# LayerNorm chains of a deformable-convolution block kept with pixels on partitions

## The chip, the cores and the metric

The kernel runs on one core of one Trainium2 chip. Its time is the device time of one execution in microseconds (us), lower is better. A time is given as the median of several runs, and one further execution was recorded by the hardware profiler.

The engines are named as in the profile: PE (TensorE matmul), PEld (its weight loads), DVE (VectorE), ACT (ScalarE), POOL (GpSimd) and SP (SyncE, which issues DMAs). PE, DVE and ACT each run their own list of instructions in order.

## What is computed

The input x is float32 of shape (2, 256, 128, 128): two images, 256 channels. Two residual layers follow each other; `_gn` is a group norm with 32 groups and no weights.

```python
def _ln2d(x, w, b):                      # over channels, at each pixel
    u = x.mean(1, keepdims=True)
    s = ((x - u) ** 2).mean(1, keepdims=True)
    return w[None, :, None, None] * (x - u) / jnp.sqrt(s + EPS) + b[None, :, None, None]

def _branch(x, w_off, w_def, lw, lb, pad, dil):
    off = _conv(x, w_off, pad, dil)              # 18 offsets at each pixel
    y = _deform_dw(x, off, w_def, pad, dil)      # 9 bilinear samples, depthwise weights
    return gelu(_ln2d(y, lw, lb))

# layer 0, on x = _gn(x)
x1, x2, x3 = (_branch(x, ..., dil) for dil in (1, 9, 12))
c = einsum('bchw,oc->bohw', x, conv_w) + conv_b
out = _ln2d(x1 + x2 + x3 + c, n1_w, n1_b)
h = gelu(out^T @ mlp_w1.T + mlp_b1) @ mlp_w2.T + mlp_b2      # 256 -> 512 -> 256
x = x_in + _ln2d(h^T + out, n2_w, n2_b)
# layer 1: x = x + 3x3 convolution of _gn(x) with ternary weights, + bias
```

In the inputs all norm weights (bw, n1_w, n2_w) are ones and all norm biases (bb, n1_b, n2_b) are zeros; conv_b, mlp_b1 and mlp_b2 are random.

## The kernel before

It has three stages. Phase A reads x, takes the first group norm's statistics, writes a padded table of pixels to DRAM, computes the offsets, and stores "hats" (the interpolation weights along y and x) in DRAM. The largest offset decides between two paths (`far`, `flag`, `beyond`): the near path `sample_near`, which these inputs take, and a general path `sample_any`, which gathers pixel by pixel with indirect DMAs. Phase C is layer 1's convolution, and neither its code nor its inputs' shapes are touched.

**Sampling.** `sample_near` walks 270 units: 2 images, 45 rows of tiles (`Rt`), 3 branches. A unit has two samples, one for each half of the 256 channels (`c`), so a row of tiles has six samples. A sample is up to 17 products of a pixel tile `xs` (126 pixels x 128 channels, the stationary operand) with a sampling matrix `A` of 216 columns or fewer (L933). Their results land in four PSUM banks `pm` (two tiles to a bank), ACT copies them to `ev` (L953, two buffers), and DVE adds them with the depthwise weights into a ring of image rows, one ring for each branch (L903). The matrix `A` of a unit is built by DVE in three steps, each a product of two hats `h` (L847); `HBUFS` hat buffers are loaded ahead on SP's queue, 567 KB each. The 17 `xs` tiles of a row of tiles are loaded on POOL's queue (L783) into `XBUFS` = NT + 6 = 23 buffers, so 6 loads of the next row can go at once, and the others wait until the current row's last sample has released its tiles.

**The tail.** When four image rows of a branch are complete in its ring, a chain begins for this group `g` of 512 pixels (`Tail.branch`). There are 64 groups, each with a chain for every branch. A chain is a Python generator: `yield n` means "go on n ticks later", and `yield n, k` also names how many of `VBUFS` tiles the chain holds then. `Tail.advance` is one tick; each sample has three, before its first product and at the tiles of `TICKS` = (5, 11). So the tail's instructions are laid between the sampling products of PE, and between ACT's copies and DVE's sums, in the order that the ticks give; `pin` keeps it.

Each chain normalises over channels in `Tail.normalised`. The data lie with channels on partitions, so it transposes eight 128x128 blocks on PE into two PSUM banks (L603, tile `tp`), lets ACT copy them to SBUF (L608, tile `T`), takes mean and variance with DVE (L616, L618), computes scale and shift with four small POOL operations (L620 to L623, tile `rs`), scales on ACT (L627, four instructions of 256 columns), and transposes the eight blocks back on PE (L639, tile `zc`). The branch then applies GELU with the norm's weights from `zc` on ACT (L655, two instructions of 512 columns). Branch 0 stores its result in DRAM (`g12d`), branch 1 adds its own (L669), and branch 2 loads the sum (`other`), loads the group's x again (`xn`), subtracts the mean on ACT (L678) and goes on in `Tail.finish`: 1x1 convolution (L583, `pc1`, products of 512 columns), sums on DVE (L695, L699), the norm with n1 (L705), the MLP's two products (L583, `hp` and `h2`) with GELU between them on ACT (L718) and the sum on DVE (L733), the norm with n2, and the residual sum (L754) with statistics for the second group norm (L758). A group so has five norms: three in the branches, two in `finish`.

All PSUM tiles of the tail (`tp`, `zc`, `pc1`, `hp`, `h2`) share one tag of four banks; with the four `pm` banks, PSUM's eight are in use. Up to `NORMS` = 3 chains may be within a norm at once.

Of the kernel before, what the change touches and what calls it, by code (L numbers as in the profile page):

```python
# [9 lines left out]
F32 = mybir.dt.float32  # L10
I32 = mybir.dt.int32
U32 = mybir.dt.uint32
BF16 = mybir.dt.bfloat16
AF = mybir.ActivationFunctionType
ALU = mybir.AluOpType
AX = mybir.AxisListType
# [3 lines left out]
P = 128  # L20
W = 128
C = 256
KC = C // P
HID = 512
MC = HID // P
R = 4
NG = R * W
# [7 lines left out]
LN_EPS = 1e-6  # L35
# [5 lines left out]
LIMIT = float(REACH)  # L41
RI, CI = 3, 8
TR, TC = RI + 2 * REACH, CI + 2 * REACH
NT = -(-(W + 2 * REACH) // CI)
# [8 lines left out]
RINGS = (9, 25, 31)  # L53
BRS = (0, 1, 2)
NORMS = 3
VBUFS = 9
PEAK = 3
GAP = 2
LAG = 5
XBUFS = NT + 6  # L60
HBUFS = 4
EBUFS = 2
TICKS = (5, 11)
XCLS = (0, 1, 4, 7)
# [10 lines left out]
def conv_preact_kernel(ctx: ExitStack, tc: tile.TileContext, t: dict, out: bass.AP):  # L75
    nc = tc.nc
    x = t["x"]
    NB, _, H, _ = x.shape
# [5 lines left out]
    const = ctx.enter_context(tc.tile_pool(name="const", bufs=1))  # L84
    scratch = ctx.enter_context(tc.tile_pool(name="scratch", bufs=1, space=DRAM))
    small = ctx.enter_context(tc.tile_pool(name="small", bufs=2))


    ident = const.tile([P, P], F32, name="ident")
# [3 lines left out]
    mhalf = const.tile([P, NG // P], F32, name="mhalf")  # L93
# [9 lines left out]
    def load_now():  # L103
        for tl, src in later:
            nc.sync.dma_start(tl, src)
        later.clear()
# [3 lines left out]
    convs = [  # L110
        load(f"convw{b}", [P, KC, C], t["convw"].rearrange("(k p) o -> p k o", p=P))
        for b in range(NB)
    ]
    negmean = [const.tile([P, KC], F32, name=f"negmean{b}") for b in range(NB)]
    w1 = load("w1", [P, KC, HID], t["w1"].rearrange("(k p) o -> p k o", p=P))
    w2 = load("w2", [P, MC, C], t["w2"].rearrange("(k p) o -> p k o", p=P))
    defw = load("defw", [P, KC, NTAP], t["defw"].rearrange("(k p) t -> p k t", p=P))
    bw = load("bw", [P, 3, KC], t["bw"])
    bb = load("bb", [P, 3, KC], t["bb"])
    b1 = load("b1", [P, MC], t["b1"])  # L120
    b2 = load("b2", [P, KC], t["b2"])
    convb = load("convb", [P, KC], t["convb"])
    n1w = load("n1w", [P, KC], t["n1w"])
    n1b = load("n1b", [P, KC], t["n1b"])
    n2w = load("n2w", [P, KC], t["n2w"])
    n2b = load("n2b", [P, KC], t["n2b"])
    l1b = load("l1b", [P, KC], t["l1b"])


    wpn = const.tile([P, 2], F32, name="wpn")  # L130
    for i, name in enumerate(("wp", "wn")):
# [8 lines left out]
    def dram(name, shape):  # L140
# [7 lines left out]
    g12d = dram("g12d", [C, HW])  # L148
    x1d = dram("x1d", [C, HW])
# [3 lines left out]
    stats2 = [  # L153
        const.tile([P, KC, NGRP, 6], F32, name=f"stats2_{b}", tag=f"stats2_{b}") for b in range(NB)
    ]
# [301 lines left out]
    with ExitStack() as actx:  # L457
        psum = actx.enter_context(tc.tile_pool(name="ps_a", bufs=1, space=PSUM))

        def gps():  # L460
            return psum.tile([P, 512], F32, name="gnps", tag="tp", bufs=2)

        ap = actx.enter_context(tc.tile_pool(name="apool", bufs=1))
        dxs = sorted({d * s for d in DILS for s in (-1, 0, 1)})
        k = {
            "dxs": dxs,
            "zero": ap.tile([P, C], F32, name="zero"),
            "wz": ap.tile([P, KC, NZ], F32, name="wz"),
            "shift": ap.tile([P, len(dxs), P], F32, name="shift"),
            "hatw": ap.tile([P, 2, NTAP * NH], BF16, name="hatw"),  # L470
            "parts": [ap.tile([P, 2, ZG, P], BF16, name=f"parts{i}") for i in range(2)],
            "zr": ap.tile([P, ZRING, NZ], F32, name="zr"),
            "planes": [ap.tile([P, 2, NG], BF16, name=f"planes{i}") for i in range(RI)],
        }
        nc.vector.memset(k["zero"], 0.0)
        for parts in k["parts"]:
            nc.vector.memset(parts, 0.0)
        XT = min(4, NGRP)
        beside = store_signs(ap)
        for b in range(NB):  # L480
            stats = ap.tile([P, KC, NGRP, 6], F32, name=f"stats1_{b}", tag=f"stats1_{b}")
            for c in range(KC):
                for g0 in range(0, NGRP, XT):
                    xt = ap.tile([P, XT * NG], F32, name="xt", tag="xt", bufs=3)
                    nc.sync.dma_start(
                        xt,
                        x[b, c * P : (c + 1) * P].rearrange("p h w -> p (h w)")[
                            :, g0 * NG : (g0 + XT) * NG
                        ],
                    )  # L490
                    for j in range(XT):
                        nc.vector.bn_stats(stats[:, c, g0 + j, :], xt[:, j * NG : (j + 1) * NG])
            if b == 0:
                load_now()
                nc.sync.dma_start(k["wz"], t["wz"].rearrange("(k p) n -> p k n", p=P))
                nc.sync.dma_start(k["shift"], t["shift"])
                hatw = ap.tile([P, 2, NTAP * NH], F32, name="hatw32", tag="xt", bufs=3)
                nc.sync.dma_start(hatw, t["hatw"])
                nc.vector.tensor_copy(k["hatw"], hatw)
                pattern = ap.tile([P, RI, NG], F32, name="pattern", tag="xt", bufs=3)  # L500
                nc.sync.dma_start(pattern[HALF : HALF + NPAT], t["pattern"])
                for i, pl in enumerate(k["planes"]):
                    nc.vector.tensor_copy(
                        pl[HALF : HALF + NPAT, 1, :], pattern[HALF : HALF + NPAT, i]
                    )
            mean, rstd = group_norm(stats, f"gn1_{b}", gps)
            gn1.append((mean, rstd))

            nc.vector.tensor_scalar(negmean[b], mean, -1.0, None, ALU.mult)
            for c in range(KC):  # L510
                nc.vector.tensor_scalar(
                    convs[b][:, c, :], convs[b][:, c, :], rstd[:, c : c + 1], None, ALU.mult
                )
            phase_a(b, ap, psum, k, beside)
        for _ in beside:
            pass


    far = small.tile([P, 1], F32, name="far", tag="far")
    nc.vector.tensor_reduce(far, amax, AX.X, ALU.max)  # L520
    farall = small.tile([P, 1], F32, name="farall", tag="farall")
    nc.gpsimd.partition_all_reduce(farall, far, P, bass.bass_isa.ReduceOp.max)
    flag = const.tile([P, 1], I32, name="flag")
# [11 lines left out]
    class Tail:  # L535
# [10 lines left out]
        def begin(self, chain, wait):  # L546
            self.waiting.append([self.now + wait, chain, 0, 1])
# [28 lines left out]
        def bank(self, name):  # L576
            return self.psum.tile([P, 512], F32, name=name, tag="tl", bufs=4)
# [67 lines left out]
        def branch(self, b, br, g, y):  # L645

            pin = self.pin
            cols = slice(g * NG, (g + 1) * NG)
            gv = g12d[b].rearrange("(k p) f -> p k f", p=P)[:, :, cols]
            z = []  # L650
            yield from self.normalised(z, y, (b, br, g))
            v = z[0]
            for c in range(KC):
                pin(
                    nc.scalar.activation(  # L655
                        v[:, c, :], z[1 + c], AF.Gelu,
                        scale=bw[:, br, c : c + 1], bias=bb[:, br, c : c + 1],
                    )
                )
            if br == 0:  # L660
                yield 2
                nc.sync.dma_start(gv, v)
                return
            yield 1, 1 + br
            other = self.tile("other")
            nc.sync.dma_start(other, gv)
            if br == 1:
                yield 2
                pin(nc.vector.tensor_tensor(v, v, other, ALU.add))  # L669
                yield 2  # L670
                nc.sync.dma_start(gv, v)
                return
            xn = self.tile("xn")
            nc.sync.dma_start(xn, x[b].rearrange("(k p) h w -> p k (h w)", p=P)[:, :, cols])
            yield 2
            for c in range(KC):
                pin(
                    nc.scalar.activation(  # L678
                        xn[:, c, :], xn[:, c, :], AF.Identity, bias=negmean[b][:, c : c + 1]
                    )  # L680
                )
            yield 1
            yield from self.finish(b, g, v, other, xn)
# [78 lines left out]
            )  # L762


    def sample_near(pool, psum, k):

        pin = tc.keep_in_program_order
        tail = Tail(pool, psum, pin)
        units = [(b, Rt, br) for b in range(NB) for Rt in range(NR) for br in BRS]
        xts, hbs, owners, begun = {}, {}, {}, set()  # L770
        done = {(b, br): 0 for b in range(NB) for br in BRS}
# [191 lines left out]
        for u, (b, Rt, br) in enumerate(units):  # L963
# [5 lines left out]
            while done[b, br] < NGRP and (  # L969
# [3 lines left out]
                g = done[b, br]  # L973
# [99 lines left out]
    with tc.If(beyond > 0) as cmp:  # L1073
        with ExitStack() as bctx:
            psum = bctx.enter_context(tc.tile_pool(name="ps_g", bufs=1, space=PSUM))
            pool = bctx.enter_context(tc.tile_pool(name="gpool", bufs=1))
            for b in range(NB):
                sample_any(b, pool, psum)
    with cmp.Else():
        with ExitStack() as bctx:  # L1080
            psum = bctx.enter_context(tc.tile_pool(name="ps_b", bufs=1, space=PSUM))
# [283 lines left out]
```

## Time and profile before

| | us |
|---|---|
| median of 3 runs | 7727.71 (7709.89 to 7749.39) |
| the profiled execution, its own time | 7750.93 |
| span of the profiled execution, first to last instruction | 7749.0 |
| phase A, about | 0 to 945 |
| sampling with the tail, about | 945 to 6702 |
| phase C, about | 6702 to 7749 |

The page's first part gives busy time, share of the span and number of instructions of each engine. A group's row gives line, engine, operation, tiles written and read, shapes and count, then its busy time and the mean length of one in ns, then the idle time of the engine just before it and what ended that. A float32 product leaves two records of PE in the trace, a transpose or a bf16 product one. Matmuls overlap in the pipe, so the mean length of one is longer than the distance from one start to the next. A row of the waits gives who waited for whom, the total in us, how many times, and the longest. A row of the windows gives the stretch, its length, the busy time of PE, PEld, DVE, ACT and POOL with counts, the granted clock of PE, the share of time that the 16 DMA engines were busy, and GB/s.

### The profile page before, as it was taken

What the parts mean: (1) busy time and instruction counts of PE and PEld (TensorE: products, weight loads), DVE (VectorE), ACT (ScalarE), POOL (GpSimd) and SP (SyncE); (2) the same over time, 40 slices, a digit from 0 to 9 for tenths busy, and PEclk for the clock granted to TensorE, in tenths of its full rate; (3) what the DMA queues carried; (4) which work ended last, traced back from release to release, by engine and by line L of the source; (5) the groups of instructions that cost most, each with busy time, mean ns of one, the idle gap of its engine ahead of it and who ended that gap; (6) DMA issues with size and microseconds to landing.
All of it is one profiled execution on the core that took longest, in us unless ns stands there. A gap on an engine that the chain in (4) does not pass through costs nothing. (4 is left out here: it accounts for less than half of the span.)

```text
span 7749.0 us, 100844 instructions
## 1 busy us (share of the span) xinstructions
PE 6963.1 (90%) x33920; PEld 5191.5 (67%) x33920; DVE 5704.2 (74%) x10502; ACT 4669.5 (60%) x9218; POOL 1673.7 (22%) x2822
## 2 busy tenths in 40 slices
PE   6899888999899989898988999899888988899999
PEld 3555587777777777777777777777777776444444
DVE  7766568787777777777577778777778776677676
ACT  2344366776777777676666777677677766433232
POOL 0000023232222332223322223322223223000000
PEclk9999989999999999999999999999999998899999
DMA  8866678777777777776678777777777775322121
GB/s 279 267 196 186 196 233 266 233 238 240 227 233 240 246 237 221 229 237 195 189 238 249 228 227 247 244 228 222 234 245 236 234 220 150 107 74 75 70 75 49
DMA packets 569469, 1596.49 MB, mean 206 GB/s; under 512 B 105408, under 2 KB 169288, under 8 KB 564712
## 3 DMA queue, kind: packets, MB, share of 16 engines
q1 hardware_dynamic: 453608, 1358.71, 55.2%
q0 software_dynamic: 97920, 197.61, 9.4%
q10 hardware_dynamic: 17408, 33.56, 1.3%
q8 instruction: 273, 4.47, 0.2%
q14 instruction: 260, 2.13, 0.1%
HBM read 1320.33 MB, written 269.20 MB: 205 GB/s over the span
## 5 line engine op out<-in xcount | busy, mean ns | idle before, releaser
L933 PE MATMUL pm<-A,xs 126*128 126x216 f32 (+3 forms) x18224 | 3540.0, 348 | 469.2 <-ACT ev L953 197.8
L933 PEld LDWEIGHTS pm<-A,xs 126*128 126x128 f32 x18224 | 3192.5, 198 | 823.6 <-ACT ev L953 342.4
L953 ACT COPY ev<-pm 128x432 f32<-128x432 f32 (+6 forms) x4824 | 2122.2, 476 | 1338.4 <-PE pm L933 1143.9
L903 DVE SCALAR_TENSOR_TENSOR ring<-ev,defw,ring 128x357 f32<-128x357 f32 (+7 forms) x4496 | 2409.8, 560 | 616.4 <-ACT ev L953 398.6
L783 POOL DMA_DIRECT2D xs<-table x1530 | 924.5, 617 | 2063.5 <-PE pm L933 1868.6
L847 DVE TENSOR_TENSOR A<-h 126x1152 f32<-126x1152 f32 (+2 forms) x756 | 1012.9, 1340 | 358.9 <-DMA h<-hats 342.0
L1216 PE MATMUL pc<-cring,signs 128*128 128x512 bf16 x4608 | 1006.0, 381 | 20.0 <-ACT cring L1163 17.4
L1216 PEld LDWEIGHTS <-signs 128*128 128x128 bf16 x4608 | 452.0, 98 | 573.3 <-issue 28.1
L627 ACT ACTIVATE T<-T,rs 128x256 f32<-128x256 f32 x1280 | 656.8, 588 | 23.9 <-POOL rs L623 23.8
L620 POOL TENSOR_SCALAR rs<-mv 128x4 f32<-128x4 f32 x320 | 133.0, 416 | 2000.4 <-DVE mv L618 1360.2
L583 PE MATMUL hp<-T,w 128*128 128x512 f32 x1024 | 484.9, 597 | 5.5 <-DVE T L754 3.3
L616 DVE BATCH_NORM_STATS2 st<-T 128x6 f32<-128x256 f32 x1280 | 446.6, 411 | 30.4 <-ACT T L608 30.0
L327 PE MATMUL pz<-wz,xa 128*128 128x486 f32 x1024 | 462.8, 581 | 3.0 <-DVE zr L334 2.9
L583 PE MATMUL h<-hT,w 128*128 128x512 f32 x1024 | 460.4, 592 | 0.0
L622 POOL TENSOR_TENSOR rs<-rs,mhalf 128x4 f32<-128x4 f32 x320 | 380.3, 1188 | 1.2
L1224 ACT ACTIVATE o<-xl,l1b 128x1024 f32<-128x1024 f32 x64 | 73.5, 1148 | 505.7 <-DMA out_x<-o 420.8
L639 PE MATMUL zc<-ident,T 128*128 128x128 f32 x2560 | 363.1, 289 | 15.8 <-ACT T L627 15.5
L583 PE MATMUL pc<-xn,convw 128*128 128x512 f32 x512 | 275.5, 688 | 103.5 <-ACT xn L678 103.5
L639 PEld LDWEIGHTS zc<-ident,T 128*128 128x128 f32 x2560 | 325.5, 151 | 61.0 <-ACT T L627 26.7
L608 ACT COPY T<-tp 128x512 f32<-128x512 f32 x640 | 341.2, 597 | 24.4 <-PE tp L603 23.8
L1163 ACT CAST cring<-D 128x2048 bf16<-128x2048 f32 (+1 forms) x140 | 245.0, 1755 | 179.6 <-PE pc L1216 124.4
L733 DVE SCALAR_TENSOR_TENSOR T<-h,b,T 128x512 f32<-128x512 f32 x128 | 96.1, 751 | 344.0 <-PE h L583 342.7
(119 smaller groups left out, 5742.4 us busy)
## 6 DMA issues: line engine op xcount, KB each, us to landing
h<-hats SPq DMA_DIRECT2D x1480, 567.0 KB
xs<-table POOLq DMA_DIRECT2D x1530, 126.0 KB, 7.5
g12d<-T SPq DMA_DIRECT2D x128, 512.0 KB
other<-g12d SPq DMA_DIRECT2D x128, 512.0 KB
hats<-hb SPq DMA_DIRECT2D x64, 720.0 KB
hats<-hb SPq DMA_DIRECT2D x64, 576.0 KB
xl<-x1d SPq DMA_DIRECT2D x56, 640.0 KB
xa<-in_x ACTq DMA_DIRECT2D x64, 512.0 KB
```

The source lines that it names most:

```text
L327: nc.tensor.matmul(pz[:, 0:NZ], lhsT=xt[:, c, r, :], rhs=k["wz"][:, c, :], start=c == 0, stop=c == KC - 1,)
L583: nc.tensor.matmul(out, lhsT=w, rhs=v, start=i == 0, stop=i == n - 1)
L616: pin(nc.vector.bn_stats(st[:, j, :], Tv[:, j, :]))
L622: nc.gpsimd.tensor_tensor(rs[:, 0, :], rs[:, 0, :], mhalf[:, 0:NB4], ALU.pow)
L627: nc.scalar.activation(Tv[:, j, :], Tv[:, j, :], AF.Identity, scale=rs[:, 0, j : j + 1], bias=rs[:, 1, j : j + 1],)
L639: nc.tensor.transpose(zc[:, j * P : (j + 1) * P], Tv[:, j, c * P : (c + 1) * P], ident)
L783: nc.gpsimd.dma_start(xt[0:TP], src)
L847: nc.vector.tensor_tensor(dst, hy[0:TP, i0:i1].rearrange("p i t w -> p t i w"), hx[0:TP, i0:i1].rearrange("p i t w -> p t i w"), ALU.mult,)
L903: pin(nc.vector.scalar_tensor_tensor(dst, src, w, dst, ALU.mult, ALU.add))
L933: nc.tensor.matmul(pm[:, j, 0:n], lhsT=xts[b, Rt][t][0:TP, c * P : (c + 1) * P], rhs=bass.AP(A.tensor, a0, [[A.ap[0][0], TP], [KA, y1 - y0 ...
L953: pin(nc.scalar.copy(dst, src))
L1216: nc.tensor.matmul(pc[:, bank, :], lhsT=w[:, m * P : (m + 1) * P], rhs=xc[:, i, k, t * JC : (t + 1) * JC, kx : kx + W], start=j == 0, stop ...
```

## The change

A class `PixelTail` takes the place of `Tail` in `sample_near`; the general path keeps `Tail`. Data that were transposed for a norm now stay with pixels on partitions until something needs channels there.

- A branch transposes its eight blocks into two banks of a tag of their own (`ln`). DVE takes the statistics from PSUM, and four ACT instructions of 256 columns apply scale, shift and GELU from the banks to an SBUF tile `v`. The copy, the transposes back and the norm's weights are left out, and one chain at a time may hold the two banks. `g12d` holds pixels on partitions, 4 KB together on each.
- The 1x1 convolution and the MLP's second product are computed in that layout (`product`): the data are the stationary operand, 128 pixels at a time, and the weights move, 256 columns. Their biases are added by a product of a 3-row matrix of ones with three bf16 rows that sum to the bias. Branch 2 adds `other` before this product.
- The norm before the MLP scales in place, then eight transposes and two ACT copies give S for the MLP's first product. The last norm scales in place, then eight transposes, and the sum with x.
- The tail's other PSUM tiles have a tag `mm` of two banks. `VBUFS` goes from 9 to 8, `XBUFS` from 23 to 22, `HBUFS` from 4 to 5.
- In phase A, `split_rows` loads the two biases and splits them. Before the choice of path, DVE tests whether bw, bb, n1w or n1b differ from ones and zeros, and if so the general path is taken.

```diff
-VBUFS = 9
-PEAK = 3
+VBUFS = 8
+PEAK = 4
...
-XBUFS = NT + 6
-HBUFS = 4
+XBUFS = NT + 5
+HBUFS = 5
...
+    ones3 = const.tile([3, P], BF16, name="ones3")
+    nc.vector.memset(ones3, 1.0)
+    row3 = const.tile([3, 2, C], BF16, name="row3")
+    convb3, b23 = row3[:, 0, :], row3[:, 1, :]
...
+    def split_rows(pool):
...
+        rows, part, sel = tmp("rows"), tmp("part", BF16), tmp("sel")
+        nc.sync.dma_start(rows, t["rows"].partition_broadcast(3))
+        nc.vector.memset(sel, 0.0)
+        for i in range(3):
+            nc.vector.tensor_copy(part, rows)
+            nc.vector.scalar_tensor_tensor(
+                sel, part, ident[0:3, i : i + 1], sel, ALU.mult, ALU.add
+            )
+            nc.vector.tensor_tensor(rows, rows, part, ALU.subtract)
+        nc.vector.tensor_copy(row3, sel)
...
+    class PixelTail(Tail):
...
+        def bank(self, name):
+            return self.psum.tile([P, 512], F32, name=name, tag="mm", bufs=2)
...
+        def product(self, name, S, bias, pairs):
+            for h in range(NG // P // 2):
+                bank = self.bank(name).rearrange("p (j c) -> p j c", c=C)
+                for j in range(2):
+                    px = slice((2 * h + j) * P, (2 * h + j + 1) * P)
+                    self.pin(
+                        nc.tensor.matmul(bank[:, j, :], lhsT=ones3, rhs=bias, start=True, stop=False)
+                    )
+                    for i, (v, w) in enumerate(pairs):
+                        self.pin(
+                            nc.tensor.matmul(
+                                bank[:, j, :], lhsT=v[:, px], rhs=w,
+                                start=False, stop=i == len(pairs) - 1,
+                            )
+                        )
+                Sh = S[:, 2 * h : 2 * h + 2, :]
+                self.pin(nc.vector.tensor_tensor(Sh, bank, Sh, ALU.add))
+                yield
...
+        def branch(self, b, br, g, y):
...
+            while self.norms:
+                yield 1
+            self.norms = 1
+            rows = []
+            for h in range(NG // P // 2):
+                tp = self.psum.tile([P, 512], F32, name="tp", tag="ln", bufs=2)
+                for j in range(2):
+                    for c in range(KC):
+                        i = j * KC + c
+                        pin(nc.tensor.transpose(tp[:, i * P : (i + 1) * P], y(c, 2 * h + j), ident))
+                    rows.append(tp[:, j * C : (j + 1) * C])
+            self.read.add((b, br, g))
+            rs = self.moments(rows)
+            yield 4, min(1 + br, 2)
...
+            self.scaled(vrows, rows, rs, AF.Gelu)
+            self.norms = 0
...
+            nc.sync.dma_start(of, gv)
...
+            yield 1, 3
+            xn = self.tile("xn")
...
+            nc.sync.dma_start(xn, xv)
+            yield 1
+            pin(nc.vector.tensor_tensor(vf, vf, of, ALU.add))
+            yield 1, 2
...
+            yield 1
+            for _ in self.product(
+                "pc1", vv, convb3, [(xn[:, c, :], convs[b][:, c, :]) for c in range(KC)]
+            ):
+                pass
+            yield 2, 1
+            rs = self.moments(vrows)
+            yield 5
+            self.scaled(vrows, vrows, rs, AF.Identity)
+            yield 2, 2
+            S = self.tile("S")
+            for c in range(KC):
+                pin(nc.scalar.copy(S[:, c, :], self.channels(vrows, c)))
...
     def sample_near(pool, psum, k):
...
-        tail = Tail(pool, psum, pin)
+        tail = PixelTail(pool, psum, pin)
```

`moments` holds the same DVE and POOL operations as `normalised` had, `scaled` the four ACT instructions, and `channels` eight transposes in two calls of four.

## The prediction

> **What bounds the kernel now.** I first read engine shares of the page, then the same busy times cut into three stretches (phase A, the sampling phase with its tail, phase C):
>
> ```profile
> PE 6963.1 (90%) x33920; PEld 5191.5 (67%) x33920; DVE 5704.2 (74%) x10502; ACT 4669.5 (60%) x9218; POOL 1673.7 (22%) x2822
> ```
>
> ```profile
> 0.00:945.00 945.00, 795.49 (x3400) 459.08 (x3400) 616.21 (x1172) 350.01 (x641) 9.69 (x21) 0.98 0.74 224
> 945.00:6702.00 5757.00, 5159.96 (x25904) 4278.93 (x25904) 4331.65 (x8455) 4001.69 (x8373) 1662.59 (x2800) 0.95 0.73 227
> 6702.00:7749.00 1047.00, 1007.61 (x4616) 453.53 (x4616) 756.30 (x877) 317.81 (x204) 1.39 (x2) 0.98 0.20 74
> ```
>
> Columns: length, then busy us of PE, PEld, DVE, ACT, POOL, the granted clock, DMA share, GB/s. The change acts in the middle stretch. There PE is busy 5160 of 5757 us (90%) and idle 597; DVE has 75%, ACT 70%. So PE work removed there should come off, unless the 597 us grow.
>
> Then the groups of the tail's layout changes, the timeline of PE where such a block stands between sampling products, and the waits:
>
> ```profile
> L627 ACT ACTIVATE T<-T,rs 128x256 f32<-128x256 f32 x1280 | 656.8, 588 | 23.9 <-POOL rs L623 23.8
> L639 PE MATMUL zc<-ident,T 128*128 128x128 f32 x2560 | 363.1, 289 | 15.8 <-ACT T L627 15.5
> L608 ACT COPY T<-tp 128x512 f32<-128x512 f32 x640 | 341.2, 597 | 24.4 <-PE tp L603 23.8
> L655 ACT ACTIVATE T<-zc,bb,bw 128x512 f32<-128x512 f32 x384 | 281.4, 793 | 29.4 <-PE zc L639 27.9
> ```
>
> ```profile
> 2500.96 3.60 PE L583 MATMUL pc<-xn,convw 128*128 128x512 f32 x8
> 2504.40 1.87 PE L933 MATMUL pm<-A,xs 126*128 126x144 f32 x10
> 2506.11 1.04 PE L603 MATMUL tp<-ident,ring 128*128 128x128 f32 x8
> 2506.98 2.36 PE L933 MATMUL pm<-A,xs 126*128 126x216 f32 x12
> 2509.17 1.04 PE L639 MATMUL zc<-ident,T 128*128 128x128 f32 x8
> ```
>
> ```profile
> DVE A L847 <- DMA h<-hats: 342.0, 132, 6.4
> PE pm L933 <- ACT ev L953: 197.8, 141, 8.3
> PE pm L933 <- DMA xs<-table: 144.7, 184, 4.2
> PE pc L583 <- ACT xn L678: 103.5, 21, 8.1
> PE pm L933 <- DVE A L847: 89.9, 40, 7.2
> ```
>
> From start to start, eight transposes hold PE 0.87 us (2506.11 to 2506.98), 0.109 each; eight records of four 512-column fp32 products 3.44 us, 0.430 each; twelve 216-column records 2.19 us, 0.183 each. The last two are both 0.84 ns a column, so at 216 columns no weight load shows. The four PE rows of the waits are 536 of the 597 idle us. Last, one row of tiles (six samples: branches 0, 1, 2, each with channel half 0 and 1), to see where idle time and transfers lie:
>
> ```profile
> 1989.66:1999.64 9.98, 9.18 (x52) 7.52 (x51) 9.14 (x28) 7.07 (x16) 5.64 (x12) 1.00 1.04 300
> 1999.64:2011.12 11.48, 7.51 (x43) 6.83 (x43) 5.90 (x9) 10.79 (x24) 5.42 (x9) 1.00 0.92 242
> 2011.12:2022.43 11.31, 11.31 (x54) 10.06 (x55) 11.03 (x21) 9.52 (x19) 0.00 (x0) 0.85 0.73 239
> 2022.43:2034.56 12.13, 12.13 (x56) 9.19 (x55) 10.34 (x21) 7.92 (x15) 1.97 (x4) 1.00 0.76 273
> 2034.56:2047.28 12.72, 12.72 (x52) 8.88 (x51) 7.40 (x11) 4.27 (x9) 0.00 (x0) 1.00 0.27 94
> 2047.28:2055.10 7.82, 7.82 (x52) 7.45 (x51) 7.31 (x15) 7.79 (x18) 5.96 (x10) 1.00 0.70 212
> ```
>
> Samples that carry little tail work on PE (last, first, second) are short, and there the DMA engines are full; branch 2, half 0, carries 7 us of tail products and its transfers rest at 0.27.
>
> **The change, part by part.** There are 64 groups of 512 pixels.
>
> PE, transposes. Each group had five norms with eight transposes there and eight back, 80. Now it has 24 for the branches, 8 for S, 8 at the end: 40. 2560 go. At 0.109 (PE in flow) that is 279 us; at 0.136, the busy time of L639 and L603 over their counts (699.5/5120), which holds stretching by waits, 349. I take 0.12: -307.
>
> PE, products. 12 products of 512 columns per group become 24 of 256: 3072 records of 0.215 instead of 1536 of 0.430, the same 660 us. New are 8 bias products per group, 512 in all, 3 rows deep, bf16, 256 columns. The chain of waits has 2247 bf16 records of 512 columns in 488.87 us, 0.218 each, so 0.109 for 256; with a whole weight load exposed (98 ns, L1216's) 0.207. That is 56 to 106 us; I take 0.12, since sampling's loads hide: +61. The Trainium skill (TensorE: Matmul & The Clock Gate, "LDWEIGHTS") says that a load's time goes by columns, not rows, so three rows cost as much as 128: 107 ns for 128 columns; if no such load hid, my estimate by that page would be +111; no row here shows a 3-row load.
>
> ACT. Per group, busy over count: a branch had 2 copies (0.533), 4 scalings (0.513), 2 GELUs (0.733), 4.6 us; now 4 GELUs of 256 columns, 0.55 at most by L627 and L655, 2.2. The first norm saves 1.4 and the last its two copies, 1.1. Together 9.7 us, 620 of ACT's 4002. None of it is on PE; it can shorten PE's 198 us of waits for ev. Bounds 0 and -198; I take -40, because many of these waits come from DVE or a transfer before ACT.
>
> DVE. The counts stay (1280 statistics; adds and evictions one for one), but 768 statistics now read PSUM. The nearest rows are a 512-column operation from PSUM (L1239, 745 ns) and from SBUF (L1196, 688): +57 ns, 44 us in all. DVE has a quarter of its time free: 0 to 44, I take +10. The Trainium skill speaks against this (VectorE: DVE Perf Modes, "Rules for kernel authors": copy PSUM to SBUF first if many operations follow); L608 gives that copy's price here, 0.533 us of ACT for two statistics that would save 0.11 of DVE.
>
> New and moved waits. Statistics wait for PE's transposes instead of ACT's copies; behind them on DVE stand the ring sums, for which ev and then PE wait. The wait goes earlier by a copy. The GELU waits for POOL's rs 4 ticks after the transposes, not 5 (540 samples have three ticks each, so a tick is 5757/1620 = 3.6 us); behind it on ACT stand ev copies, and PE's four pm banks cover eight tiles. Before, that wait was 23.8 us. 0 to 100, +10. In the built order POOL now issues the last 12 tile loads of a row in one block, where rs operations stood between them; a rs waits up to 12 x 0.6 us behind it, and the last load goes out earlier. Products and back-transposes share two banks instead of four; in the built order nearly all reuses have at least 2 us of PE work between, against 0.75 for an eviction: 0 to 70, +5. The `other` load of branch 2 is queued on SP one tick before xn instead of beside it, its sum moves before the product; xn keeps its two ticks, so I leave its 103.5 us as they are.
>
> Buffers. One xs buffer less: twelve loads of a row, not eleven, wait for the last sample's releases, one issue later (0.6 us), 90 rows: 0 to 54; POOL's block gives some back: +20. One hat buffer more: 0 to -90 (PE's wait for A); -30.
>
> Transfers. In the built order the products sit in branch 0 half 1 to branch 1 half 1; branch 2 half 0 holds none. So bare samples are now branch 2's two and branch 0's first, about 22 us. Before, they were the last and the next row's first two: 212 x 7.82 + 300 x 9.98 + 242 x 11.48 = 7.4 MB in 29.3 us of that row. The new three build four of nine hat steps where the old built five, and five buffers may be drained. 0 to +423 (worked out below); I take +25, near the lower end.
>
> Phase A. The bias rows are split by 11 DVE operations of 512 elements (0.4 to 0.75 us) and a small load, in front of the z evictions, and hatw's load waits for their buffers: 0 to 20, +10. The test for other norm weights is 7 operations of 0.16 us.
>
> Sum: -307 + 61 - 40 + 10 + 10 + 5 + 20 - 30 + 25 + 10 = -236. The profiled execution took 7750.93 us (span 7749.0), which gives 7515. It is 23 above the median of the runs, 7727.71; by that, 7492.
>
> **The rivals.** (1) *Absorbed*: DVE or the bare samples set the pace, and half of the 246 us returns as PE idle time, 1.4 us a row. For: DVE is at 75% of a stretch that shrinks, with 342 us lost to hats already. Against: PE had no idle time in four of the six samples shown. 7600 to 7700. (2) *Slower*: the bare samples are bound by transfers. If they must move the same 7.4 MB at the shown mean of 254 GB/s, three samples last 29.3 us instead of 22; less the 2.6 us a row already idle for xs and A ((144.7 + 89.9)/90), that is +4.7 a row, +423 in 90 rows. Without the 25 booked above, 7727.71 - 261 + 423 = 7890. It decides from 261/90 = 2.9 us a row. Against it: fewer hats to build there, and one buffer more. (3) *Better*: waits for ev and A mostly vanish (-200): about 7350. (4) The test sends it down the general path: 27648 gathers at 0.6 us, over 16 ms; the weights are ones and zeros, so hardly.
>
> **How the numbers follow.** Forecast 0.60 (7410 to 7600), better 0.13, absorbed 0.20 (0.05 of it within 0.5%), slower 0.06, general path 0.01. Faster 0.88, same 0.05, slower 0.07; 0.5% is about what this measurement can tell from no change. For eight in ten I go from 7390 to 7640.
>
> **What would show it.** PE busy in the middle stretch near 4910, its idle time 560 to 620; ACT near 3380 and DVE near 4370 there; bias records near 0.12 from start to start; xs waits not over 170. PE idle over 800 would make it wrong, as would 256-column records over 0.23.

## The result, and the profile after

The changed kernel took 7953.34 us (median of four runs, 7938.30 to 7968.76) against 7733.28 us for the kernel before: 1.0287 times, with a 95% interval of 1.0252 to 1.0322. The prediction, 7492 us, was 461 us too low and had the wrong sign.

The profiled execution took 7938.3 us, span 7936.4. Phase A is no longer than before (the first sampling product starts at 935.5 us; before, at 946.5) and phase C is as long as before, so the loss lies in sampling. First the engine shares and the three stretches (columns as before: length, busy us of PE, PEld, DVE, ACT, POOL, granted clock, DMA share, GB/s):

```profile
PE 7046.5 (89%) x33408; PEld 5319.3 (67%) x33408; DVE 5690.1 (72%) x10521; ACT 4100.7 (52%) x8194; POOL 1630.5 (21%) x2822
```

```profile
0.00:955.00 955.00, 801.21 (x3436) 465.37 (x3436) 625.27 (x1193) 351.56 (x650) 16.33 (x32) 0.97 0.75 227
955.00:6880.00 5925.00, 5233.80 (x25350) 4398.52 (x25349) 4303.39 (x8443) 3428.20 (x7336) 1612.79 (x2788) 0.92 0.75 219
6880.00:7936.00 1056.00, 1011.47 (x4625) 455.42 (x4624) 761.47 (x886) 320.92 (x210) 1.39 (x2) 0.98 0.20 75
```

ACT lost 573 us of work (620 were forecast), and 2560 transposes are gone, but PE's busy time rose by 74 us, its idle time by 94 (597 to 691), and the granted clock fell from 0.95 to 0.92. Next, the waits:

```profile
ACT v L833 <- POOL rs L826: 556.5, 156, 20.7
PE pm L1152 <- ACT ev L1172: 376.1, 218, 12.7
PE pm L1152 <- DMA xs<-table: 230.2, 326, 3.2
DVE A L1066 <- DMA h<-hats: 180.8, 77, 8.2
```

PE's waits for ev and for tiles were 198 and 145 us; ACT's wait for rs was 24. Then the windows of one row of tiles, sample by sample:

```profile
1954.66:1972.01 17.35, 12.17 (x53) 10.18 (x51) 11.64 (x18) 10.40 (x23) 7.91 (x14) 0.81 0.97 277
1972.01:1986.03 14.02, 14.02 (x56) 10.86 (x56) 7.80 (x18) 7.25 (x14) 1.67 (x4) 0.87 0.70 206
1986.03:2002.37 16.34, 16.34 (x75) 12.99 (x74) 11.21 (x17) 8.16 (x16) 0.00 (x0) 1.00 0.72 209
2002.37:2014.42 12.05, 12.05 (x63) 10.01 (x62) 10.01 (x24) 5.98 (x12) 1.66 (x4) 1.00 0.49 139
2014.42:2020.27 5.85, 5.85 (x36) 5.85 (x34) 5.82 (x19) 4.11 (x9) 1.67 (x4) 1.00 0.60 201
2020.27:2027.92 7.65, 6.99 (x45) 6.74 (x44) 7.54 (x18) 6.33 (x16) 5.73 (x8) 1.00 0.73 224
```

The tail's products are now in the second to fourth samples, because a branch's chain got shorter by some ticks while LAG stayed 5. The bare samples are branch 2's two and the next row's first, and that first sample takes 17 us at clock 0.81 with 5 us of idle PE. The timeline at another row boundary shows why. The new row's tile loads are on POOL, and the `rs` operations of two norms are among them:

```profile
2091.16 0.23 POOL L823 TENSOR_SCALAR rs<-mv 128x4 f32<-128x4 f32 x1
...
2093.31 0.34 POOL L826 TENSOR_TENSOR rs<-rs 128x4 f32<-128x4 f32 x1
...
2093.83 4.87 POOL L1002 DMA_DIRECT2D xs<-table  x8 [0.17 <-PE pm L1152]
...
2102.57 0.59 POOL L1002 DMA_DIRECT2D xs<-table  x1 [3.87 <-PE pm L1152]
...
2106.68 0.60 PE L1152 MATMUL pm<-A,xs 126*128 126x216 f32 x2 [1.14 <-DMA xs<-table]
...
2107.12 0.59 POOL L1002 DMA_DIRECT2D xs<-table  x1 [0.80 <-DVE stats L977]
2107.80 0.38 POOL L823 TENSOR_SCALAR rs<-mv 128x4 f32<-128x4 f32 x1
...
2109.81 1.93 ACT L833 ACTIVATE v<-tp,rs 128x256 f32<-128x256 f32 x4 [5.33 <-POOL rs L826]
```

The loads hold up `rs` (until 2107.80), so ACT stands 5.33 us in front of its GELUs, and ev copies queue behind them. The loads are late in turn: a first block of `rs` (2091.16 to 2093.65) stands among them, and the last four stop four times, for 6.65 us together. So the last one is issued at 2107.12, and PE waits for its tiles.

The table gives the mean length of each sample (b0 h0 is branch 0, half 0) over the rows away from the images' edges, and, over the sampling stage, PE's waits for ev and xs and its **half-clock time**. The trace gives the granted clock as stretches of 1 or 0.5; half-clock time is the sum of those at 0.5.

| | b0 h0 | b0 h1 | b1 h0 | b1 h1 | b2 h0 | b2 h1 | ev | xs | half clock |
|---|---|---|---|---|---|---|---|---|---|
| before | 10.0 | 9.3 | 11.2 | 11.5 | 15.2 | 7.3 | 200 | 148 | 578 |
| changed | 16.3 | 11.8 | 13.2 | 10.9 | 5.9 | 7.8 | 377 | 234 | 931 |
| LAG 11, old buffers (e10) | 7.9 | 9.0 | 10.2 | 11.5 | 13.2 | 11.5 | 346 | 96 | 555 |
| LAG 11, NT + 9 (e14) | 6.4 | 9.3 | 10.2 | 11.7 | 13.2 | 11.6 | 378 | 13 | 472 |
| no rs, NT + 9 (e18) | 11.1 | 13.3 | 13.9 | 10.6 | 5.9 | 8.4 | 213 | 24 | 540 |

In the changed kernel's b0 h0, 5.0 of the 16.3 us are idle time of PE, 2.7 for tiles and 2.3 for ev, and 6.1 us are at half clock; before, 1.6 us were idle and 0.6 at half clock. The DMA engines are 0.97 busy there, and were 0.98 busy before.

PE's time from start to start, idle time taken out, from the first sampling product to the tail's last transpose, closes the account (us, before to changed): transposes 610 to 363 (-247); bias products +108; products of 256 columns 705 to 765 (+60); `hp` +6; sampling products 3401 to 3561 (+160, the same 18224 records); idle +110. Sum +197, the growth of the stage.

### The profile page after: what moved, and what is told of

It reads as the page before. It is cut to its first block, busy times and chain, and to the rows that moved or that the text cites. A ratio compares the mean times of both kernels' runs of the same rounds, so it can differ in the third digit from the quotient of the medians.

```text
span 7936.4 us, 98143 instructions
## 1 busy us (share of the span) xinstructions
PE 7046.5 (89%) x33408; PEld 5319.3 (67%) x33408; DVE 5690.1 (72%) x10521; ACT 4100.7 (52%) x8194; POOL 1630.5 (21%) x2822
## 5 line engine op out<-in xcount | busy, mean ns | idle before, releaser
L1152 PE MATMUL pm<-A,xs 126*128 126x216 f32 (+3 forms) x18224 | 3655.9, 355 | 648.7 <-ACT ev L1172 376.1
L833 ACT ACTIVATE v<-tp,rs 128x256 f32<-128x256 f32 x768 | 371.6, 567 | 329.6 <-POOL rs L826 329.5
L854 PE MATMUL h<-w,hT 128*128 128x256 f32 x2048 | 510.5, 392 | 0.0
L619 PE MATMUL hp<-S,w 128*128 128x512 f32 x1024 | 489.4, 603 | 18.0 <-ACT S L935 14.5
L854 PEld LDWEIGHTS h<-w,hT 128*128 128x128 f32 x2048 | 368.0, 189 | 70.4
L833 ACT ACTIVATE v<-v,rs 128x256 f32<-128x256 f32 x512 | 265.7, 592 | 227.0 <-POOL rs L826 227.0
L1113 ACT ACTIVATE ring<-ev,defw 128x384 f32<-128x384 f32 (+2 forms) x604 | 332.1, 566 | 16.3
L854 PE MATMUL pc<-convw,xn 128*128 128x256 f32 x1024 | 306.1, 423 | 17.6 <-ACT xn L919 17.6
L944 ACT ACTIVATE hT<-hp,b 128x512 f32<-128x512 f32 x256 | 176.0, 688 | 275.3 <-PE hp L619 274.3
L860 DVE TENSOR_TENSOR v<-h,v 128x512 f32<-128x512 f32 x128 | 88.2, 689 | 315.7 <-PE h L854 312.0
```

Source lines behind the costliest of these rows:

```text
L619: nc.tensor.matmul(out, lhsT=w, rhs=v, start=i == 0, stop=i == n - 1)
L833: nc.scalar.activation(dst[j], src[j], func, scale=rs[:, 0, j : j + 1], bias=rs[:, 1, j : j + 1])
L854: nc.tensor.matmul(bank[:, j, :], lhsT=v[:, px], rhs=w, start=False, stop=i == len(pairs) - 1,)
L1113: pin(nc.scalar.mul(dst, src, w))
L1152: nc.tensor.matmul(pm[:, j, 0:n], lhsT=xts[b, Rt][t][0:TP, c * P : (c + 1) * P], rhs=bass.AP(A.tensor, a0, [[A.ap[0][0], TP], [KA, y1 - y0 ...
```

## The experiments

The theories: **P**, `rs` stands behind tile loads on POOL, so ACT and ev are late; **B**, the place of the bare samples makes them outrun their tile loads; **W**, a bias product costs much more than 0.12 us. The kernel before took 7733 to 7742 us in all comparisons; ratios are to it, with 95% intervals. Unless said otherwise an edit is made to the changed kernel.

**The order on POOL (e1).** POOL's instructions are kept in program order: the loads that need a release stand right behind the product that frees the tile, and `rs` where the chain issues it.

```diff
-nc.gpsimd.tensor_scalar(rs[:, 0, :], ...)          # and the other three
+pin(nc.gpsimd.tensor_scalar(rs[:, 0, :], ...))
+if br == BRS[-1] and c == KC - 1:                  # within the sample
+    load_some(len(ts))
```

> The changed kernel, with POOL's instructions in program order: the first five tile loads of the next row of tiles go after branch 1's first sample, each of the other twelve right after the sampling product that frees its buffer, and the rs operations where their ticks put them. Nothing else differs. Theory P (rs stands behind a block of tile loads on POOL, ACT waits for rs, so ev is not copied, PE runs out of pm banks and its clock falls): ACT's waits for rs fall from 556 us to under 150, PE's waits for ev from 376 to under 200, the clock in branch 0's first sample comes back from 0.81 to over 0.93, and the time is 7600 to 7780. Theory B (branch 2's bare samples outrun the transfers, whatever POOL's order): tile loads land as late as before, PE's waits for xs stay at 200 or more, time 7880 to 8000.

8290.55 us, 1.0713 [1.069, 1.0737]. ACT's waits for rs fell to 80 us and PE's for ev to 241, but those for tiles rose to 566:

```profile
PE pm L1159 <- DMA xs<-table: 566.4, 513, 9.4
PE pm L1159 <- ACT ev L1181: 240.8, 194, 4.5
ACT v L833 <- POOL rs L826: 80.4, 31, 20.7
```

Branch 0 half 0 took 22 us. P's remedy made the loads late: `rs` alone doesn't set this sample.

**The place of the tail's work (e2, e5).**

```diff
-LAG = 5
+LAG = 14          # e2; 11 in e5
```

> The changed kernel with LAG = 14 instead of 5: the same tail work, three samples later, so that PE's tail products stand in branch 2's two samples and the next row's first one, where tile loads arrive, and branch 0's second to branch 1's second sample are bare. Theory B: PE's waits for xs fall from 230 us to under 80 and those for ev to under 200, time 7550 to 7720. Theory P: the rs operations meet tile loads at other places and POOL is scheduled anew, so it may help or not, but ACT's waits for rs stay over 300 us and the time over 7800.

7872.81 us, 1.0185 [1.0155, 1.0216]: waits for tiles 79 us, but those for ev stay at 320, and there are new ones, 166 us for xn. B's time was missed by over 150 us.

> Only the wait before a chain's start changes (LAG 5 to 11), so that the heavy tail products lie in branch 1 half 1, branch 2 half 0 and branch 2 half 1, about where the kernel before had them, and the bare samples are branch 0's two and branch 1's first. B (the place of the bare samples against the tile loads): branch 0, half 0 comes back from 16.3 us to 10 to 12, xs waits from 234 to 100 to 170 us, the granted clock in that sample over 0.95; time 7800 to 7850, with the bias products' 148 us as most of what is left. P (rs behind the block of tile loads): POOL's order is as before in kind, so ACT still waits over 400 us for rs, and the time is within 40 us of 7953.

7885.67 us, 1.0194 [1.0155, 1.0233]. Branch 0 half 0 took 10.8 us, as B said, but tiles still cost 267 us. Place alone is worth 68 us, less than B forecast.

**The bias products (e3, e6).** Left out (the first line taken away, nothing in its place), and issued once for each bank:

```diff
-for j in range(2): matmul(bank[:, j, :], lhsT=ones3, rhs=bias, start=True, stop=False)
+matmul(bank, lhsT=ones3, rhs=twice, start=True, stop=False)     # bias row read twice, 512 columns
```

> The changed kernel without the 512 bias products: the 1x1 convolution's and the second MLP product's biases are left out. By the prediction's price (0.12 us each) 61 us less, 7890. By what the trace has for the product itself (0.212 from start to start) 108 us less, 7845. If each also exposes its own weight load before it (0.41 in all, as eight 256-column records between two of them last 1.92 us instead of 1.71) 210 us less, 7740. If branch 0's first sample is what sets the pace and PE's work elsewhere is covered, under 30 us less.

> One bias product of 512 columns for each bank instead of two of 256: 256 records instead of 512, the same columns, the same result. W (the price is the record's, above all its weight load between float32 products, about 0.2 us of 0.4): 256 x 0.2 = 51 us less, 7900. Rival (the price goes by columns, or by the wait for the bank): no change, within 15 us of 7953.

7805.33 us, 1.0087 [1.006, 1.0114], and 7905.59 us, 1.021 [1.0167, 1.0253]: -148 and -48 us. W holds. The timeline of PE in the changed kernel shows the price:

```profile
1991.74 0.28 PE L850 MATMUL h<-row,ones 3*128 3x256 bf16 x1
1991.95 1.99 PE L854 MATMUL h<-w,hT 128*128 128x256 f32 x8
1993.87 0.28 PE L850 MATMUL h<-row,ones 3*128 3x256 bf16 x1
```

A bias product takes 0.21 us from start to start, and the eight records behind it 1.92 us, against 8 x 0.216 = 1.73 without bias (e3). So each costs 0.4 us.

**The buffers (e4, e8).** As before, and with three tile buffers more.

```diff
-XBUFS = NT + 5
-HBUFS = 5
+XBUFS = NT + 6          # e4; NT + 9 in e8
+HBUFS = 4
```

> The changed kernel with the buffers of the kernel before: 23 xs buffers instead of 22, 4 hat buffers instead of 5. If the lost xs buffer makes the tile loads late (one issue later in each of 90 rows, 0.6 us): 40 to 80 us less, waits for xs from 230 to about 150. If the hat buffer is worth what the waits for A lost (90 to 3 us): 50 to 90 us more. Theories P and B: within 40 us of 7953.

7923.32 us, 1.0217 [1.0176, 1.0258]: 30 us back, hardly more than the noise (its interval touches that of the changed kernel).

> Four tile buffers more (NT + 9) and one hat buffer less (4). So 9 of a row's 17 loads can go before the last sample, and 8 wait for its releases instead of 12. B (late tiles): xs waits fall from 234 to under 120 us, branch 0, half 0 from 16.3 to about 13 us, time 7800 to 7870, well below the 7923 of NT + 6. P: the block of loads in front of rs is only a third shorter; 7900 or more.

7904.18 us, 1.0215 [1.0177, 1.0253]. The waits for tiles are gone and those for ev have taken their place:

```profile
PE pm L1152 <- ACT ev L1172: 579.6, 234, 9.1
PE pm L1152 <- DMA xs<-table: 65.0, 69, 17.2
```

**rs by itself (e7, e9, e17).** GELU 7 ticks after the statistics instead of 4; tile loads on SP's queue; constants in place of `rs`.

```diff
-yield 4, min(1 + br, 2)
+yield 7, min(1 + br, 2)                  # e7
-nc.gpsimd.dma_start(xt[0:TP], src)
+nc.sync.dma_start(xt[0:TP], src)         # e9
-nc.gpsimd.tensor_scalar(rs[:, 0, :], ...)          # and the other three
-return rs
+return rs0                               # e17: a tile that is set once
```

> A branch's GELUs come 7 ticks after its statistics instead of 4, nothing else. P: ACT's waits for rs fall from 557 us to under 150, PE's waits for ev from 377 to about 250, and the time by 100 to 130 us, to about 7840. B: the waits for rs fall too, but they were not what set branch 0, half 0; that sample stays over 15 us and the time is within 40 us of 7953.

8095.84 us, 1.0457 [1.0419, 1.0495]: ev fell to 119 us, yet the chain now holds its two banks longer and moves, and PE waits elsewhere:

```profile
PE tp L887 <- ACT v L833: 284.2, 241, 5.3
PE pc L854 <- ACT xn L919: 283.2, 24, 21.5
```

> The tile loads are issued on SP's queue instead of POOL's; nothing but rs is left on POOL. P (rs behind tile loads): ACT's waits for rs fall from 557 us to under 60, PE's waits for ev from 377 to 150 to 200, and the time by 100 to 200 us, to 7750 to 7850. B (tile loads are late whichever queue issues them): the waits for rs go too, but xs waits stay over 200 us, branch 0 half 0 stays over 14 us, and the time is within 60 us of 7953; hats and the tail's own loads, now queued behind a block of 12 tile loads on SP, may add waits for A and xn.

8165.75 us, 1.0546 [1.0482, 1.061]. Waits for tiles are gone, but the tail's own loads stand behind the block of tile loads on SP:

```profile
PE pm L1152 <- ACT ev L1172: 405.9, 216, 18.6
PE zc L868 <- DVE xr L973: 225.4, 73, 8.6
PE pc L854 <- ACT xn L919: 219.5, 30, 14.7
```

> The changed kernel with constants in place of rs: the four POOL operations of each norm are left out, and scale and shift in the result are wrong; ACT then waits neither for POOL nor for DVE's statistics. P: waits for ev fall from 377 to under 200 us, branch 0 half 0 from 16.3 to about 13 us, time 7780 to 7850. B (late tiles and half clock): xs waits stay over 200 us and half-clock time over 800 us, the time is within 60 us of 7953.

7826.63 us, 1.0125 [1.0085, 1.0165]: 127 us less, within P's range, with ev at 197 and xs still at 250 us. Branch 0 half 0 still took 15.3 us, not the 13 of P, and half-clock time was 797 us. A row's last load went out 3.1 us after its first sample began (median), against 3.6 in the changed kernel, so `rs` alone doesn't make the loads late. This takes away ACT's wait for DVE's statistics too, so P's share is at most that.

**Both at once (e18).** Constants for `rs`, and NT + 9 with 4.

> Constants in place of rs as in the run before, and NT + 9 tile buffers with 4 hat buffers. If rs and late tiles together are the row boundary's cost at LAG 5: waits for xs and ev together under 250 us (610 in the changed kernel, 629 with the buffers alone), half-clock time under 600 us, time 7600 to 7700, near the 7607 of LAG 11 with these buffers. If the place of the tail's work costs in a third way (DVE or ACT behind after three bare samples): 7800 to 7900.

7630.13 us, 0.986 [0.9818, 0.9903]. Alone the two edits gave 127 and 49 us; together they give 323. The waits for ev and xs together, 611 us in the changed kernel, are 450 in e17, 646 in e8 and 237 here: each had been the other's next bound. Here the place is still that of the changed kernel. The clock has a part in it: of the 289 us by which the sampling stage is shorter, 78 are idle time of PE, and half-clock time fell by 391 us, which at half the speed is up to 195 us. A new wait, for A, has come up:

```profile
PE pm L1149 <- ACT ev L1169: 211.2, 209, 3.4
PE pm L1149 <- DVE A L1063: 166.0, 37, 8.4
PE pm L1149 <- DMA xs<-table: 23.7, 37, 2.0
```

**Place and buffers at once (e10, e11, e13, e14, e15).** LAG 11 with the buffers of before; the same without bias products; with HBUFS 4 alone taken back; with NT + 9 and 4; and that with one bias product for each bank.

```diff
-LAG = 5
+LAG = 11
-XBUFS = NT + 5          # e13
+XBUFS = NT + 6          # e10, e11; NT + 9 in e14, e15
-HBUFS = 5
+HBUFS = 4
```

> LAG 11 together with the buffers of the kernel before (XBUFS NT + 6, HBUFS 4): placement and buffers of the kernel before, tail of the changed one. If placement and buffers are the whole cause of the added stalls, xs and ev waits come back to about 350 us together, PE's time at half clock in this stage to about 600 us (before 578, after 931), and the time to 7700 to 7780. If the two only add up as measured alone (68 and 30 us): 7855.

7699.04 us, 0.9955 [0.9928, 0.9982]: 254 us back, where the parts alone gave 68 and 30. The changed tail, with the buffers of the tail before and near its place (one sample later in the row), is 40 us faster than it. One row of it:

```profile
1936.84:1943.04 6.20, 6.20 (x35) 6.20 (x34) 6.13 (x21) 3.97 (x8) 5.42 (x11) 1.00 0.98 261
1943.04:1949.25 6.21, 6.21 (x36) 6.21 (x35) 6.05 (x11) 5.33 (x12) 2.93 (x4) 1.00 0.83 249
1949.25:1961.77 12.52, 8.54 (x51) 7.71 (x51) 10.07 (x16) 10.47 (x23) 0.00 (x0) 1.00 0.59 209
```

The row's first sample has the same sampling products as the 17.35 us one and takes 6.20, no idle time, at full clock. The DMA engines are as full (0.98) as there, so full DMA engines alone do not stretch this sample.

> As the run before, and without the bias products (the two biases are then missing from the result). If the price of the bias products is independent of the stalls, 148 us less than that run: 7560 to 7630 if placement and buffers are the whole cause, 7707 if they only add up. Rival (PE work taken out comes back as waits, since transfers or DVE set the row's time): less than 75 us below that run.

7606.85 us, 0.9836 [0.9783, 0.989], 92 us less than e10: between the two expectations. PE's time for bias products and their neighbours is 191 us less, but sampling products take 48 more (half-clock time 555 to 680) and idle time grows by 42.

> LAG 11 with XBUFS NT + 5 as in the changed kernel and HBUFS 4 as before: of the two buffer edits only the hat buffer is taken back. If the fifth hat buffer is what hurts with that placement (hats loaded further ahead share the transfers with the late tiles): 7700 to 7730, xs waits about 100 us. If the missing tile buffer is what hurts: 7860 to 7900, xs waits about 270 us.

7754.22 us, 1.0015 [0.9996, 1.0034]. From e5, 131 of the 187 us came from the hat buffer and 55 from the tile buffer: both.

> LAG 11, HBUFS 4 and three tile buffers more, NT + 9 in place of NT + 6. If late tiles still bind at the row boundary: xs waits from 96 to under 30 us, half-clock time under 500 us, time 7630 to 7670. Rival (waits for ev take their place, as with these buffers at LAG 5): within 20 us of 7699.

> As the run before, with one bias product of 512 columns for each bank in place of two of 256: 40 to 50 us less than that run, as much as at LAG 5 (48); 7590 to 7620 if the tile buffers bring what they may, 7650 if they bring nothing.

7606.59 us, 0.9838 [0.9794, 0.9882], and 7519.92 us, 0.9733 [0.9687, 0.9778]: 92 and another 87 us, both more than expected. e15 is the fastest version, 2.7% below the kernel before. With NT + 9, eight loads of a row are left for the last sample. In the median row they go out 0.6 us apart without a stop, and none of the eight ever waits for an earlier load to land. With twelve, the last four do: 41 times in the changed kernel, 57 us in all (most of the other 123 such waits of POOL stand before the next row's first five loads).

**The clock (e12).** Nine products more in every branch 0 half 0, into banks that are then overwritten.

```diff
+if br == BRS[0] and c == 0:
+    pin(nc.tensor.matmul(pm[:, 0, 0:n], lhsT=ident[0:TP, 0:P], rhs=..., start=True, stop=True))
```

> Nine products more in each branch 0 half 0 (identity as stationary operand, the sampling matrix moving, into the bank that the real product then overwrites; the result stays the same): about 3.1 us of PE work at full clock in each of 90 samples, 280 us in all. Clock theory (idle PE has its clock halved for 3.4 us at a time, and that is what stretches this sample): half-clock time falls well below 931 us, the sampling records there get shorter, and the time changes by less than 60 us either way. Rival (PE's idle time is all there is to it, or PE work is simply added): 150 to 280 us slower, with half-clock time unchanged.

7992.80 us, 1.0335 [1.0275, 1.0395]. 346 us of work on PE cost 39 us: half-clock time fell from 931 to 560 us and a sampling record from 195 to 185 ns, some 180 us over 18224 records; idle time of PE fell by 93 us. So PE's idle time does bring the half clock here, and the half clock costs time; the sample itself, with the added work, still took 17.0 us.

**The place in the old tail (e16).** In the kernel before:

```diff
-LAG = 5
+LAG = 2
```

> The kernel before with LAG 2 in place of 5, nothing else: its tail's products lie one sample earlier in a row, so that branch 2's two samples and branch 0's first are the bare ones, as in the changed kernel. If that place is a cause of its own: branch 0 half 0 from 10.0 to 13 to 16 us, half-clock time from 578 to over 750 us, and the time 100 to 200 us above before, 7840 to 7940. Rival (it hurts only with the changed tail or its buffers): within 40 us of 7739.

8011.26 us, 1.0353 [1.0307, 1.04]. Branch 0 half 0 took 14.6 us and half-clock time was 833 us, as the theory of the place said. But the time is longer than it expected, for a new wait came with it: the chains start before DVE has summed their rows.

```profile
PE tp L603 <- DVE ring L903: 378.7, 169, 8.9
PE pm L933 <- DMA xs<-table: 170.3, 253, 2.8
```

That the place would hurt the old tail without this wait stays open.

## Why the prediction was wrong

**The step that failed is the term for transfers and bare samples,** +25 out of 0 to +423. The prediction saw in the built order that branch 2's samples and branch 0's first would be bare, priced it in rival 2 at up to +423, and then took the low end, on the ground that fewer hats are built there and that there is a fifth hat buffer. With the old buffers, going from LAG 5 (e4) to LAG 11 (e10) is worth 224 us, 2.5 us a row; the rival said it would decide from 2.9. With the changed kernel's buffers it is worth 68 us (e5), with NT + 9 and 4 it is 298 (e8 to e14).

Rival 2 came near the time, 7890, but partly by luck, for it gave the tail's edits 261 us and the bare samples 423. The three samples now take 16.3 + 5.9 + 7.8 = 30.0 us, and it had 29.3. Its reason doesn't hold as it stands: it let the three samples move a fixed 7.4 MB at a mean rate. In e18, with the bare samples at the same place, they take 25.4 us and carry 5.8 MB in the mean row, against 7.0 MB in the changed kernel; the kernel's total is 1596 MB in both.

What differs between the runs is when the loads go out. Counted from the start of the row's first sample, the last load goes out 3.6 us after it in the changed kernel (median), 0.8 us before it in e10, 2.1 before it in e18 and 6.0 before it in e14. A late load also takes long to land, 10.7 us in the changed kernel against 5.5 in e10 and 7.2 in e14, while the DMA engines are 0.97 busy. The late issue is shown; how much of the delay is the filled DMA engines' stays open.

**The waits for rs** were booked at +10 of 0 to 100 and are worth up to 127 (e17). The block of twelve loads was named, and so was the queue behind ACT; but each wait was priced as if the other were not there. e17, e8 and e18 show that they hang together.

**The clock was in no term.** The sum took durations from a stage with clock 0.95 and no bound for a lower one. Half-clock time grew by 353 us; at half the speed that is up to 177 us of PE time, against +160 in the sampling products.

The other terms, by e10 against before where the stalls are alike:

- Transposes, -307: -267 (2560 left at 0.134 us, not 0.119); -247 in the changed kernel, where `zc` takes 0.178.
- Bias, +61: 107 for the products alone and 84 more in the float32 products behind them (e10 against e11); 92 to 148 us of time. That sampling's products hide its weight load was wrong: it stands between the tail's own products. The side estimate by the Trainium skill (TensorE: Matmul & The Clock Gate, "LDWEIGHTS (loading the stationary operand)"), +111, agrees with the 107 and leaves out the neighbours.
- Products of 256 columns, no change: right; without bias they take 673 us, against 705.
- ACT, -620 of busy time: -573, right. That it shortens waits for ev by 40 was wrong: they are 146 us longer in e10, while those for xn and tiles are 94 and 52 shorter; all idle time is +35.
- DVE, +10: right. Statistics from PSUM take 417 ns, from SBUF 411.
- Buffers, +20 - 30: the hat buffer was booked as a gain and is a loss, 131 us at LAG 11. With the old ones 30 us come back at LAG 5, 187 at LAG 11.
- Phase A, +10: not seen.

Taken in this order, the tail's edits are worth 40 us (before to e10) where 261 were booked, the place costs 224 (e10 to e4) where 25 were, and the buffers cost 30 (e4 to changed) where a gain of 10 was booked: misses of 221 + 199 + 40 = 460 us. Less the 10 booked for phase A, that is 450 of the miss of 461. In the other order the buffers cost 187 (e10 to e5) and the place 68 (e5 to changed); only the two together, 254 us where 15 were booked, do not depend on it. Of the signs named ahead, PE's busy time (5234, not 4910), the waits for xs (230, not under 170), the bias records (0.21, not 0.12) and the 256-column records (0.235, over 0.23) showed it wrong.

## What to carry to other kernels

A chain that gets shorter moves its work in time: when the place of the work is set by a delay in ticks, tune that delay and the buffers again before judging the change. Two streams on one in-order queue, here small operations that others wait for and loads that wait for releases, should be priced together, since taking away either wait alone may only bring out the other. Count, too, how many loads a block holds: here the ones after the eighth were the late ones. Where PE idles for half of a few microseconds, add the halved clock to the price.

## What the runs showed of the hardware

The granted clock has two levels here, and its stretches at half are multiples of 3.41 us. In the changed kernel, 125 of the 130 stretches follow 3.41 us in which PE was idle for over 1.5 us in all; of the 1303 other such windows at full clock none was idle for over 1.92 us, and most had no idle time. Between 1.5 and 1.92 us it went either way: 36 windows before a half-clock stretch, 31 not. The longest single gap in those 125 windows was as short as 0.70 us. The Trainium skill (TensorE: Matmul & The Clock Gate, "HAM oscillation — how this bites in real kernels") has as its rule no idle gaps over about 3.4 us; by this trace many short ones that add up to nearly half of a window do the same.

In all 19 traces with the tile loads on POOL, a load never went out while more than seven earlier tile loads were still in flight. A block of up to eight can thus go out without a stop, as in e14; one of twelve stops where a load takes over some 4.8 us to land (eight issues of 0.6 us; an estimate).
